# Ten node-range places in one register load on VectorE: a graph layer on one Trainium2 core

## The chip, the core and the metric

The kernel runs on one core of a Trainium2 chip. Its engines work side by side, each from an instruction stream of its own, in order: TensorE (PE in the profile, with its weight loads as PEld), VectorE (DVE), ScalarE (ACT), GpSimd (POOL), and SyncE (SP), which here only issues DMA transfers. Each engine has a sequencer that fetches its instructions. Some instructions are the sequencer's own work and never reach the engine's arithmetic: loading a number from memory into a register, register arithmetic, and tests on registers. The profile shows those of DVE under the name DVEq and doesn't count them as busy time. Engines wait for one another by semaphores.

The metric is the device time of one execution in microseconds (us), of which the median of several runs is given. The profile is of one further execution, with a span counted from its first to its last instruction.

## The reference, cut to what matters

```
Xs  = x[src]                                       # 400,000 edges, 12,500 nodes, 128 features
msg = where(edge_type == 0, Xs @ W_data.T + b_data, Xs @ W_control.T + b_control)
agg = segment_sum(msg, dst, 12500)                 # dst is sorted
x   = layernorm(x + relu(agg + (x @ W_self.T + b_self)))
```

A row of `x` is fetched for every edge, the rows are summed by destination node, separately for the two edge types, and the sums go through the weights. The kernel sums first and multiplies by the weights after, and it counts the edges of each type and node, since each brings one bias.

## The kernel before

**Tiling.** The edges come in 3125 chunks of 128, and 125 chunks make a group. There are 25 groups. A group covers some 500 destination nodes, and a group's chunks fall into five windows of 25 chunks. In a window 5 chunks are gathered: POOL issues one indirect transfer for each chunk (`msg`, line 793). The other 20 chunks are picked: `x` lies in SBUF as three bf16 parts, and TensorE fetches the edges' rows by multiplying with matrices of zeros and ones (`got`, line 893), which ACT copies to SBUF as bf16 (`emsg`, line 907). In 18 of the groups the last window is gathered as a whole, so the kernel has 107 picked sets in all, here called rounds, and 125 gathered ones.

**Summing.** TensorE multiplies the fetched rows with a selection matrix that DVE makes by comparison (`esel` for picked rows, three pieces of 1760, 1584 and 1056 columns for each round; `psel` for gathered ones; both at line 516, in the helper `select`). The product is a tile `sums` in PSUM (line 738), of which there are two. Its columns are a narrow range of destination nodes for either edge type. A tile for gathered rows also has the counts (line 824).

**Adding up.** DVE adds `sums` into `acc`, a tile of 128 x 3 x 640 fp32 for each group, at line 782 (`accumulate`). The columns of `acc` at which a window's range begins depend on the data. These are the places: ten numbers for each group, five for gathered and five for picked ranges, of which the groups with four rounds use nine. They are worked out on the chip for all groups near the start, held between 0 and 520 by a max and a min (lines 405 and 406), and lie as whole numbers in one partition of SBUF (`place_i`, `raw["place"]`). `place_of(g, i)` at lines 772 to 776 loads one of them into a register of DVE. `accumulate` uses that register as part of its addresses. A gathered window has two additions: the counts (64x120) as soon as they are there, and the sums (128x2x40 or, where all 25 chunks are gathered, 128x2x120) at the window's end. A picked round has one (128x2x88).

**The rest of DVE's round.** For the round two ahead DVE works out where its edges stand: `O` (line 516), `ahead` (613), `prod` (617, 622), `found` (624), `rank` (626), `rm` (516), `rv` (657), `key` and MAX8 (630, 634), `om_all` (541), and `pick` (724), the matrix with which TensorE picks. Once a group, index tiles are prepared (`parts`, `pk`, lines 494 to 498) and the nodes of a group that is complete are multiplied by the weights and normalized (lines 1012 to 1045). Line 766 carries the overlap of `acc` on to the next group.

**What sets the order.** `merged` and `evenly` give each piece of work a place in a round, and the pieces are recorded in that order. The layer that records them then orders the instructions of each engine anew, by what it reckons of when their operands are ready. `tc.issue_after(ins)` holds an instruction behind another of its engine in that order: a place's load stands behind the last addition but one that was recorded before it. POOL's gathers are paced by TensorE's progress (`paced`).

After the main part every engine loads one number (`bad`, line 118) and skips a slow path that covers unlikely data.

Of the kernel before, what the change touches and what calls it, by code (L numbers as in the profile page):

```python
# [39 lines left out]
WMAX = max(AW, EW)  # L40
CHUNKS = PB + EC
M0 = 50
R = 640
# [16 lines left out]
def kernel(  # L60
# [53 lines left out]
    with ExitStack() as sx:  # L114
        short_path(sx, tc, const, ident, eps, wT, brow, bad, x, src, dst, etype,
                   (w_data, w_ctrl, w_self), (b_data, b_ctrl, b_self), out)
# [89 lines left out]
def short_path(ctx, tc, const, ident, eps, wT, brow, bad, x, src, dst, etype, ws, bs, out):  # L206
    nc = tc.nc
# [32 lines left out]
    raw = {}  # L240
# [484 lines left out]
        return [(0.6, lambda: half(0, NCELL))]  # L725


    acc, added, parts_in = {}, [], {}

    def sums():  # L730
        return ps2.tile([P, 512], FP, name="sums")
# [40 lines left out]
    def place_of(g, i):  # L772

        parts_in[g] = parts_in.get(g, 0) + 1
        with tc.issue_after(added[-2].ins) if len(added) > 1 else ExitStack():
            return nc.vector.value_load(raw["place"][0:1, g, i:i + 1], min_val=0, max_val=R - WMAX)  # L776

    def accumulate(at, rows, ps, wide, width):

# [49 lines left out]
    def gathered(g, i):  # L829
# [3 lines left out]
        def add_counts():  # L833
            s["at"] = place_of(g, 2 * i)
            accumulate(s["at"], acc_rows(g, 2, 3)[:2 * CAP], s["ps"][:2 * CAP, 2 * AW:], AW, AW)
# [37 lines left out]
    def picked(w, tiled, ending, before):  # L873
# [83 lines left out]
        def end():  # L957

            early, *more = tiled.get(turns, [lambda: None])
            early()  # L960
            gates = add(bounds[turns - 1], NQ)
            for u in more:
                u()
            accumulate(place_of(g, 2 * i + 1), acc_rows(g, 0, 2), s["ps"], EW, EW)
            return gates
# [174 lines left out]
    for w in range(pairs):  # L1140
        g, i = each_e[w]
# [182 lines left out]
```

## Time and profile before

| | |
|---|---|
| time, median of 3 runs | 1736.49 us (1736.48 to 1737.98) |
| the profiled execution | 1736.82 us, span 1735.1 us |
| PE busy | 1585.6 us, 91% of the span |
| DVE busy | 1559.6 us, 90% |
| ACT busy | 1228.9 us, 71% |
| POOL busy | 1243.4 us, 72% |
| TensorE clock granted | 0.998 |
| DMA | 252.35 MB, mean 145 GB/s |

The shares are means over the whole span. The first 60 us are a start-up with little work for PE (7.63 us busy), and the last 23 us an ending (14.23 us); between them each stretch of 200 us looks like the next. A busy engine isn't one that sets the time: what bounds the kernel is read from who waits for whom. In the tables of groups, a row has the line, engine, operation, tiles and shape with the count, then the busy time in us and the mean of one in ns, then the idle time of the engine before them and what ended it. In the tables of waits a row has who waited for what, the total in us, the number of times and the longest. In the table of one line's instructions, the three numbers are the shortest, median and longest in ns.

### The profile page before, as it was taken

The numbers are of one execution on the slowest core, as the hardware profiler recorded it, in microseconds if no ns is written. First come the engines' busy times: TensorE is split into PE (matmuls) and PEld (weight loads), VectorE is DVE, ScalarE is ACT, GpSimd is POOL, SyncE is SP. The second block draws the span as 40 slices with busy tenths as digits, with TensorE's granted clock in tenths as the row PEclk, the third lists the DMA queues.
The fourth block names the chain that finished last, engine by engine and source line by source line (L and its number), as shares of the span: only waits on it lengthen the run. The fifth ranks groups of instructions, "written<-read, shape, count | busy, mean of one in ns | idle before, by whom it ended". The sixth has DMA issues, their size and how long they took to land.

```text
span 1735.1 us, 67976 instructions
## 1 busy us (share of the span) xinstructions
PE 1585.6 (91%) x28250; PEld 1249.1 (72%) x28250; DVE 1559.6 (90%) x3642; ACT 1228.9 (71%) x2201; POOL 1243.4 (72%) x1059
## 2 busy tenths in 40 slices
PE   1699999999999999999999999999999999999997
PEld 0477777777677777777777777777777777777776
DVE  7898999999999999999898999899999898999983
ACT  5777777767777676767677777776777676777675
POOL 1276778877778776767787777776777777777671
PEclk9999999999999999999999999999999999999999
DMA  7844454555454454444545444544454544444441
GB/s 221 275 135 137 130 155 127 159 153 149 124 158 130 139 159 147 134 144 135 151 125 169 138 149 130 159 130 154 139 162 124 161 129 146 146 154 126 136 134 46
DMA packets 145646, 252.35 MB, mean 145 GB/s; under 512 B 35563, under 2 KB 111936, under 8 KB 145328
## 3 DMA queue, kind: packets, MB, share of 16 engines
q1 hardware_dynamic: 82670, 138.54, 23.6%
q0 software_dynamic: 50032, 102.98, 22.3%
q10 hardware_dynamic: 12626, 6.40, 1.3%
q8 instruction: 223, 3.65, 0.9%
q14 instruction: 95, 0.78, 0.1%
HBM read 230.17 MB, written 17.67 MB: 143 GB/s over the span
## 4 chain that ended last, share of the span: by engine, by line
DVE 43%; PE 39%; issue 9%; ACT 5%; DVEq 2%; DMA 2%; SPq 0%; ACTq 0%
PE sums L738 17%; PE got L893 13%; DVE esel L516 5%; DVE prod L622 4%; DVE pick L724 3%; DVE prod L617 3%; PE side L1012 3%; DVE rv L657 3%; DVE found L624 2%; DVE psel L516 2%; DVE prod L595 2%; DVE acc L782 2%; ACT emsg L907 2%; DVE O L516 2%; DVEq L776 2%
## 5 line engine op out<-in xcount | busy, mean ns | idle before, releaser
L793 POOL DMA_INDIRECT msg<-rows,idx_g x985 | 1174.3, 1192 | 361.6 <-issue 128.6
L907 ACT CAST emsg<-got 128x768 bf16<-128x768 f32 (+1 forms) x1070 | 953.7, 931 | 360.1 <-PE got L893 338.4
L738 PE MATMUL sums<-esel,emsg 128*128 128x176 bf16 x7704 | 686.6, 240 | 0.6 <-ACT emsg L907 0.4
L738 PEld LDWEIGHTS <-emsg 128*128 128x128 bf16 x7704 | 566.0, 98 | 102.8 <-issue 95.5
L893 PE MATMUL got<-x,pick 128*32 128x384 bf16 x10486 | 584.8, 330 | 15.2 <-DVE pick L724 9.7
L893 PEld LDWEIGHTS <-pick 128*32 128x32 bf16 x10486 | 239.7, 96 | 135.0 <-DVE pick L724 12.1
L516 DVE TENSOR_TENSOR esel<-code_col,code 128x1760 bf16<-128x1760 bf16 x321 | 293.0, 913 | 16.2 <-PE sums L738 14.9
L738 PE MATMUL sums<-psel,msg 128*128 128x48 bf16 x2955 | 183.6, 184 | 31.3 <-DVE acc L782 29.3
L738 PEld LDWEIGHTS <-msg 128*128 128x128 bf16 x2955 | 153.8, 97 | 62.4 <-issue 58.3
L622 DVE TENSOR_TENSOR prod<-prod 128x1200 bf16<-128x1200 bf16 x214 | 133.7, 625 | 4.7
L516 DVE TENSOR_TENSOR O<-cell_col,blk 128x2000 bf16<-128x2000 bf16 x107 | 127.6, 1193 | 8.2 <-ACT blk L420 3.7
L617 DVE TENSOR_TENSOR prod<-O,ahead 128x2000 bf16<-128x2000 bf16 x107 | 128.4, 1200 | 5.8 <-DVE ahead L613 3.5
L782 DVE TENSOR_TENSOR acc<-acc,sums 128x80 f32 (+3 forms) x357 | 98.9, 280 | 32.4 <-PE sums L738 29.8
L516 DVE TENSOR_TENSOR psel<-near_col,near 128x1200 bf16<-128x1200 bf16 x125 | 97.4, 779 | 23.1 <-issue 22.4
L724 DVE TENSOR_SCALAR pick<-pick,lane_f 128x3200 bf16<-128x3200 bf16 x107 | 112.8, 1054 | 0.6 <-DMA pick<-there 0.6
L868 POOL DMA_INDIRECT both<-rows,idx x54 | 63.4, 1174 | 64.6 <-ACT emsg L907 27.0
L669 PE MATMUL side<-rv,O 128*128 128x64 bf16 x2140 | 83.6, 195 | 23.0 <-DVE rv L657 21.5
L669 PEld LDWEIGHTS <-O 128*128 128x128 bf16 x2140 | 78.8, 100 | 24.9 <-DVE rv L657 21.8
L657 DVE TENSOR_TENSOR rv<-rm,vals 128x1280 bf16<-128x1280 bf16 x107 | 87.8, 820 | 0.0
L624 DVE TENSOR_REDUCE found<-prod 128x20 f32<-128x600 bf16 x107 | 83.0, 776 | 5.2 <-DVE prod L622 2.7
L595 DVE TENSOR_TENSOR prod<-O 128x1000 bf16<-128x1000 bf16 x107 | 71.8, 671 | 0.0
L605 PEld LDWEIGHTS <-ltri 128*128 128x128 bf16 x1284 | 40.4, 97 | 36.3 <-issue 34.5
(171 smaller groups left out, 1536.2 us busy)
## 6 DMA issues: line engine op xcount, KB each, us to landing
pick<-there SPq DMA_DIRECT2D x106, 800.0 KB
acc<-acc_start SPq DMA_DIRECT2D x23, 960.0 KB
msg<-rows,idx_g POOLq DMA_INDIRECT x985
rows<-x SPq DMA_DIRECT2D x6, 1344.0 KB
xs<-in_x_dram SPq DMA_DIRECT2D x99, 62.5 KB
out_dram<-h SPq DMA_DIRECT2D x99, 62.5 KB
xt<-in_x_dram ACTq DMA_DIRECT2D x6, 896.0 KB
there<-cell SPq DMA_DIRECT2D x106, 6.2 KB
```

Source lines behind the costliest of these rows:

```text
L516: nc.vector.tensor_tensor(sel.rearrange("p n (w t) -> p n w t", t=2), col[:rows].rearrange("p (o w t) -> p o w t", o=1, t=2).to_broadcast( ...
L617: nc.vector.tensor_tensor(prod[:, :, :NCELL], s["O"], ahead.rearrange("p (o j) -> p o j", o=1).to_broadcast([P, EC, NCELL]), op=OP.mult,)
L622: nc.vector.tensor_add(prod[:, :, :h], prod[:, :, :h], prod[:, :, h:2 * h])
L624: nc.vector.tensor_reduce(found, prod[:, :, :h], AX.X, OP.add)
L657: placed[:] = [nc.vector.tensor_tensor(rv.rearrange("p c v (r t) -> p c v r t", t=2), rm.rearrange("p c (o r t) -> p c o r t", o=1, t=2).t ...
L669: nc.tensor.matmul(s["rk"][:m, :2 * CAP], s["held"][:, c * NCELL:c * NCELL + m], s["rv"][:, c].rearrange("p v r -> p (v r)"), start=(c == ...
L724: nc.vector.tensor_scalar(t, t, lane_f, None, op0=OP.is_equal)
L738: last = nc.tensor.matmul(out, msg[:, j * D:(j + 1) * D], sel, start=(start and j == 0), stop=stop, skip_group_check=True)
L782: added.append(nc.vector.tensor_add(win, win, ps[:, :n * wide].rearrange("p (a w) -> p a w", w=wide)[:, :, :width]))
L793: return nc.gpsimd.indirect_dma_start(out=msg, out_offset=None, in_=rows3[:, :], in_offset=bass.IndirectOffsetOnAxis(ap=codes["p", g][0][: ...
L893: last = nc.tensor.matmul(ps[CAP * a:CAP * (a + 1), :], slots[w]["pick"][:, a * NQ + q, :], x3[:, 4 * q + a - a0].rearrange("p j d -> p (j ...
L907: s["out"] = nc.scalar.copy(msg[:, :n], ps[:, :n, :3 * D])
```

## The change

`place_of` loads a group's ten places with one instruction the first time that a place of this group is asked for, and keeps the ten registers. Later calls for the group load nothing. The instructions that test at run time whether a place lies between 0 and 520 are left out. Only the first call for a group is held behind an addition, by the same rule as before. The additions and their addresses are as they were.

```diff
-    acc, added, parts_in = {}, [], {}
+    acc, added, parts_in, at_places = {}, [], {}, {}
...
     def place_of(g, i):
 
         parts_in[g] = parts_in.get(g, 0) + 1
-        with tc.issue_after(added[-2].ins) if len(added) > 1 else ExitStack():
-            return nc.vector.value_load(raw["place"][0:1, g, i:i + 1], min_val=0, max_val=R - WMAX)
+        if g not in at_places:
+            with tc.issue_after(added[-2].ins) if len(added) > 1 else ExitStack():
+                _, at_places[g] = nc.values_load_multi_w_load_instructions(
+                    raw["place"][0:1, g, :], engines=[nc.vector.engine], min_val=0, max_val=R - WMAX,
+                    skip_runtime_bounds_check_because="places are held to this range by a max and a min on the chip",
+                )
+        return at_places[g][i]
```

The lines behind the edit move down by five: what was line 782 is line 787 in the changed kernel, and the load is at line 777.

## The prediction

> **What bounds the kernel now.** First the page's head, the busy times and the chain that ended last, then two stretches of the steady part.
>
> ```profile
> span 1735.1 us, 67976 instructions
> PE 1585.6 (91%) x28250; PEld 1249.1 (72%) x28250; DVE 1559.6 (90%) x3642; ACT 1228.9 (71%) x2201; POOL 1243.4 (72%) x1059
> DVE 43%; PE 39%; issue 9%; ACT 5%; DVEq 2%; DMA 2%; SPq 0%; ACTq 0%
> PE sums L738 17%; PE got L893 13%; DVE esel L516 5%; DVE prod L622 4%; DVE pick L724 3%; DVE prod L617 3%; PE side L1012 3%; DVE rv L657 3%; DVE found L624 2%; DVE psel L516 2%; DVE prod L595 2%; DVE acc L782 2%; ACT emsg L907 2%; DVE O L516 2%; DVEq L776 2%
> ```
> ```profile
> 400.00:600.00 200.00, 188.15 (x3362) 147.08 (x3359) 181.18 (x422) 140.93 (x262) 150.53 (x126) 1.00 0.48 143
> 1000.00:1200.00 200.00, 188.24 (x3398) 148.89 (x3396) 183.80 (x422) 142.09 (x259) 151.11 (x127) 1.00 0.46 140
> ```
>
> After its length, a stretch's row gives PE, PEld, DVE, ACT and POOL. PE is busy for 188 of 200 us and DVE for 181 to 184: two engines that are both nearly full and hand work to each other. The chain takes 43% from DVE and 39% from PE, so each is the late one about as often. ACT and POOL have a quarter of their time free. The line that the change edits, L776, stands on the chain itself with 2% (about 30 us): DVE's sequencer, which fetches DVE's instructions and does the register work, loading places.
>
> Next, what DVE waited for. "<- issue" is idle time for which the profile shows no other work to wait for.
>
> ```profile
> DVE acc L782 <- PE sums L738: 29.8, 51, 1.3
> DVE ahead L613 <- PE side L605: 26.0, 48, 2.0
> DVE psel L516 <- issue: 22.4, 43, 1.5
> DVE esel L516 <- PE sums L738: 14.9, 23, 2.6
> DVE prod L617 <- DVE ahead L613: 3.5, 10, 0.7
> DVE found L624 <- DVE prod L622: 2.7, 12, 0.2
> DVE x L293 <- issue: 2.5, 1, 2.5
> DVE parts L494 <- issue: 2.3, 5, 0.5
> DVE O L516 <- issue: 2.2, 4, 0.7
> DVE rm L516 <- DVE rank L626: 1.0, 2, 0.5
> DVE acc L782 <- issue: 0.9, 2, 0.5
> ```
>
> And the reverse, PE waiting for DVE in the steady part:
>
> ```profile
> PE sums L738 <- DVE acc L782: 29.5, 53, 1.5
> PE side L545 <- DVE om_all L541: 16.8, 26, 1.6
> PE side L487 <- DVE code_r L477: 13.7, 18, 1.2
> PE got L893 <- DVE pick L724: 9.7, 13, 1.5
> ```
>
> PE's largest wait is for the addition at L782: there are two `sums` tiles in PSUM, and PE can begin a new set only when DVE has added an old one into `acc`. These rows give 69.7 us of PE waiting for DVE, against 70.7 us (29.8 + 26.0 + 14.9) of DVE waiting for PE. So I count a stall of DVE, added or taken away, at half: about half of the time the other engine would have been the late one anyway.
>
> **What goes: 232 loads and their tests.** The instructions of L776, and the address arithmetic of L782, which stays:
>
> ```profile
> L776 DVEq TENSOR_LOAD <-place_i x232: 296/304/1402, 42.1 to 1721.3; - x116
> L776 DVEq FUSED_REGOPS  x232: 183/190/206, 43.4 to 1721.7; - x116
> L776 DVEq SEQ_ASSERT  x232: 23/23/31, 43.6 to 1721.9; - x116
> L782 DVEq FUSED_REGOPS  x357: 69/75/117, 78.1 to 1722.8; - x179
> ```
>
> A place costs the sequencer 304 + 190 + 23 = 517 ns and the gaps between, in which it dispatches nothing. DVE goes on with what it has been given and then stands. What that looks like:
>
> ```profile
> 498.70 0.16 DVE L1038 SCALAR_TENSOR_TENSOR nm<-mv,rs 125x4 f32<-125x4 f32 x1
> 500.05 0.78 DVE L516 TENSOR_TENSOR psel<-near_col,near 128x1200 bf16<-128x1200 bf16 x1 [1.19 <-issue]
> ```
>
> Two places were loaded here behind one instruction of 0.16 us: 1.19 us idle, so about 0.66 us each with gaps. Over the whole kernel the idle time that fits is the issue rows (22.4 + 2.5 + 2.3 + 2.2 + 0.9 = 30.3) and the three short rows in which DVE waited for itself although a load stood between (3.5 + 2.7 + 1.0 = 7.2): 37.5 us. The ends are 0, if PE is always next, and 37.5; 2% of the chain lies between. By the half: **-19 us**. What is late next is PE's product, on which the same additions and selections wait.
>
> **What comes: 25 loads of ten.** In the order of the built program one load stands for each of the 25 groups, with no test behind it. Its price is in no row. Ends: 0.304 us, if ten registers cost what one does, and 3.04 us, if each costs the whole. I take the sequencer's shortest register instruction (the 75 ns of L782) as the share paid once and the rest of the 304 as paid per register: 0.075 + 10 x 0.229 = 2.37 us. That is nearer the upper end, because the one-register row is all but constant (296 to 304 in half of the cases, far above 75), which looks like a trip to memory and back rather than like decoding.
>
> The Trainium skill ("Runtime: NRT & Kernel Launch", section on instruction fetch mechanics) has a register load at some 200 ns per register even in bulk; by it, as an estimate, ten cost 304 + 9 x 200 = 2.1 us, and the time below would be 1750. The traced load of one register, 304 ns, fits that rule with 100 ns paid once but does not prove it.
>
> Where the new loads stand matters more. The old ones were spread over the stream; each new one is directly ahead of its group's first addition. In the built order 12 of them stand ahead of the 64x120 addition, which takes the counts out of `sums`, and 13 ahead of the 128x2x88 addition. Behind the load are queued the address arithmetic, that addition, and DVE's next selection; PE waits for the addition (the 29.5 us row). What covers a load is the instruction ahead of it:
>
> ```profile
> L516 DVE TENSOR_TENSOR O<-cell_col,blk 128x2000 bf16<-128x2000 bf16 x107 | 127.6, 1193 | 8.2 <-ACT blk L420 3.7 <-issue 2.2 <-ACT emsg L907 1.2
> L516 DVE TENSOR_TENSOR esel<-code_col,code 128x1760 bf16<-128x1760 bf16 x107 | 113.6, 1061 | 7.1 <-PE sums L738 6.7
> L516 DVE TENSOR_TENSOR esel<-code_col,code 128x1584 bf16<-128x1584 bf16 x107 | 104.3, 974 | 0.4
> L624 DVE TENSOR_REDUCE found<-prod 128x20 f32<-128x600 bf16 x107 | 83.0, 776 | 5.2 <-DVE prod L622 2.7
> L541 DVE TENSOR_SCALAR om_all<-slot_col,side 128x448 bf16<-128x448 bf16 x107 | 42.9, 440 | 1.0 <-PE side L535 0.5
> L782 DVE TENSOR_TENSOR acc<-acc,sums 128x176 f32 x107 | 35.5, 332 | 25.8 <-PE sums L738 24.9 <-issue 0.5
> L498 DVE SCALAR_TENSOR_TENSOR pk<-idx_g,vals 128x125 f32<-128x125 int32 x25 | 7.0, 280 | 0.0
> L634 DVE MAX8 top<-key 128x8 f32<-128x20 f32 x107 | 18.2, 171 | 0.6
> L516 DVE TENSOR_TENSOR esel<-code_col,code 128x1056 bf16<-128x1056 bf16 x107 | 75.3, 704 | 8.8 <-PE sums L738 8.1
> ```
>
> The built order has ahead of the loads six O, six MAX8, three found, three om_all, two pk, two selections of 1584, one of 1760, one addition of 332 ns and one tiny instruction: 7.16 + 1.03 + 2.33 + 1.32 + 0.56 + 1.95 + 1.06 + 0.33, 15.7 us over 25, or 0.63 us each. The addition would also have waited for PE for 29.8 / 357 = 0.08 us. Exposed: 2.37 - 0.71 = 1.66 us, times 25 is 41.5 us on DVE, half of it **+21 us**. The ends are 0 (at 0.304 us all is covered) and 25 x (3.04 - 0.71) = 58 us.
>
> The test of the range that is dropped was work of the sequencer only, counted above. DMA issues and the queues of SP and POOL keep their instructions; POOL's order differs in two places and SP's in some 70, with transfers loaded far ahead of use: nothing.
>
> **What moves.** Taking 232 loads out lets the layer that orders the instructions arrange all of DVE anew: beside the loads, 1524 of 4421 rows of DVE's order stand elsewhere, by up to 19 places. DVE is in order, so a row that stands ahead of its time holds everything behind it. Three shifts can be counted. The third selection (128x1056), which needs a tile that PE is still reading, stands ahead of its round's `found` in 31 rounds instead of 12, and behind the nearest `pick` in 31 instead of 18, where PE is kept waiting for it: 32 shifts. The 64x120 addition stands directly behind `rm` or `found`, well ahead of its old place, in 21 cases instead of 6. At the mean of one such wait in the rows above (14.9 / 23 = 0.65 us for a selection, 29.8 / 51 = 0.58 us for an addition) that is 32 x 0.65 + 15 x 0.58 = 29.5 us, half of it **+15 us**. A gain cannot be excluded, since the new order could as well serve PE better elsewhere; ends -15 (the same size, the other way) and +30 (passed on in full).
>
> **Sum.** -19 + 21 + 15 = +17 us on the profiled execution's 1736.82 us; the median of the runs is 1736.49, 0.3 below, so 1753.5 us, 1.0% slower.
>
> **The rivals.**
>
> *A load of ten costs little more than a load of one.* Place: the 25 loads. Then they are covered, and the sum is -19 + 15 = -4, 1733 us; with an order that costs nothing, 1718. It decides below the price at which 25 x (L - 0.71) / 2 equals 4, L = 1.03 us. For it: nothing in the trace says that the 304 ns are per register. Against: they are far above the 75 ns of pure register work. The Trainium skill ("DMA: Bandwidth & Descriptors", latency and other measured facts) gives a tensor load a floor of some 600 ns that unrolling spreads, which would speak for this rival; the trace's 304 ns is half of that floor.
>
> *The new stalls pass in full.* PE stands for just that addition, so a late one may delay PE by all of it: -19 + 41.5 + 15, 1774 us. For it: the 29.5 us row is PE's largest wait. Against: it was 53 waits in 357 additions.
>
> *The order costs nothing.* Waits change place without adding up: -19 + 21 = +2, 1739 us. For it: the counted shifts are a few among 1524.
>
> That the change does less than it says is excluded: the built program has 25 loads at that line, no tests, and the same 3642 instructions of DVE proper.
>
> **How the numbers follow.** Chances: forecast 0.55, its own range 1744 to 1766; cheap load 0.23; full passing 0.12; neutral order 0.10. Of the cheap load's 0.23, 0.13 end faster by over 0.2% (3.5 us, about what a measurement of this kernel can tell from no change), 0.06 within, 0.04 slower. The neutral order splits into 0.02, 0.05 and 0.03; of the forecast 0.01 is within. Faster 0.15, same 0.12, slower 0.73. The range from 1731 to 1774 leaves out the cheap load with a good order below (about 0.12) and part of the full passing above (0.06).
>
> **What will show it.** L776's rows shrink to 25 loads without register operations or tests; their median is the price: near 2.4 us if I am right, under 1.0 if the first rival is. The "psel <- issue" row disappears. DVE's busy sum stays at 1560. PE's wait for the addition grows from 29.5 us, DVE's wait for PE at the 128x1056 selection from 8.1 us. If both of these stay and the load is long, the order term was wrong; if DVE's idle time falls and the time with it, the half was too little for the gain.

## The result, and the profile after

The changed kernel takes 1754.96 us, the median of 4 runs (1754.22 to 1755.82), against 1736.95 us (1736.48 to 1737.98) for the kernel before: a ratio of 1.0104, 95% interval 1.0091 to 1.0118. It is about 18 us slower, and the forecast was 1753.5.

The head of the changed kernel's page and the shares of its chain by engine (the profiled execution took 1755.82 us):

```profile
span 1754.1 us, 67306 instructions
PE 1602.5 (91%) x28250; PEld 1254.1 (71%) x28250; DVE 1556.9 (89%) x3642; ACT 1229.5 (70%) x2201; POOL 1261.2 (72%) x1059
PE 43%; DVE 38%; issue 7%; ACT 5%; DMA 1%; POOL 1%; DVEq 1%; ACTq 0%; POOLq 0%
```

DVE has 2.7 us less work than before in a span that is 19 us longer, so it stands still longer: span less busy time was 175.5 us and is 197.2. The sequencer's share of the chain (DVEq) has fallen from 2% to 1%.

TensorE's row holds a surprise. Span less busy time was 149.5 us for PE and is 151.6, hardly more, while its busy time grew by 16.9 us at the same 28250 matmuls. The means of its two largest groups are as before (240 ns for the sums of picked rows, 330 ns for `got`), so the matmuls overlap less. PE takes them in another order now; the ends of matmuls are modelled in the profile, so a stall shorter than a matmul can also stand as busy time. The granted clock, 0.998 before and 0.995 after, would make some 5 us of it if the busy time went with it (0.3% of 1585.6, an estimate).

What is left at the line of the load, first all 25 of them, then three neighbours, each from a window of its own:

```profile
L777 DVEq TENSOR_LOAD <-place_i x25: 1061/2296/2629, 78.4 to 1677.8; - x25
...
L777 DVEq TENSOR_LOAD <-place_i x1: 2317/2317/2317, 1344.3 to 1344.3; - x1
L777 DVEq TENSOR_LOAD <-place_i x1: 1064/1064/1064, 1409.6 to 1409.6; - x1
L777 DVEq TENSOR_LOAD <-place_i x1: 2300/2300/2300, 1472.2 to 1472.2; - x1
```

There are 25 loads of ten registers, and no tests. But they have two prices. From the second load on they alternate all through the kernel: 2.30 us for groups 1, 3, 5 and so on, 1.07 us for 2, 4, 6. (Group 0's ten are among the cheap ones by their place; its load took 2.63 us here and 1.64 in another execution.)

What DVE waited for in the changed kernel:

```profile
DVE acc L787 <- PE sums L738: 53.6, 71, 1.9
DVE ahead L613 <- PE side L605: 29.0, 52, 2.0
DVE esel L516 <- PE sums L738: 26.1, 38, 1.9
...
DVE acc L787 <- issue: 8.8, 8, 2.4
```

"psel <- issue", 22.4 us before, is gone with the old loads. In its place the additions wait 53.6 us for PE (29.8 before) and the selections 26.1 (14.9), and 8.8 us stand as "issue" ahead of additions, in seven of the eight cases behind a new load that was not covered in full. What PE waited for:

```profile
PE sums L738 <- DVE acc L787: 41.7, 56, 1.9
...
PE side L545 <- DVE om_all L541: 9.6, 17, 1.6
```

PE's wait for the additions grew from 29.5 to 41.7 us. The groups of DVE where the idle time went, by shape (busy us, mean ns, idle before them):

```profile
L516 DVE TENSOR_TENSOR esel<-code_col,code 128x1056 bf16<-128x1056 bf16 x107 | 75.4, 705 | 19.3 <-PE sums L738 18.1 <-PE side L487 0.7 <-PE got L898 0.3
L516 DVE TENSOR_TENSOR psel<-near_col,near 128x1200 bf16<-128x1200 bf16 x125 | 96.3, 770 | 0.0
L787 DVE TENSOR_TENSOR acc<-acc,sums 128x176 f32 x107 | 35.7, 333 | 46.4 <-PE sums L738 37.4 <-PE got L898 5.6 <-issue 2.9
L787 DVE TENSOR_TENSOR acc<-acc,sums 64x120 f32 x125 | 32.9, 263 | 11.7 <-issue 5.9 <-PE sums L738 3.1 <-PE side L690 2.4
```

The means are within about one per cent of those before. The 128x1056 selection now stands 19.3 us idle (8.8 before), the 128x176 addition 46.4 (25.8).

### The profile page after: what moved, and what is told of

Same layout as the page of the kernel before. It is cut to its first block, busy times and chain, and to the rows that moved or that the text cites. A ratio compares the mean times of both kernels' runs of the same rounds, so it can differ in the third digit from the quotient of the medians.

```text
span 1754.1 us, 67306 instructions
## 1 busy us (share of the span) xinstructions
PE 1602.5 (91%) x28250; PEld 1254.1 (71%) x28250; DVE 1556.9 (89%) x3642; ACT 1229.5 (70%) x2201; POOL 1261.2 (72%) x1059
## 4 chain that ended last, share of the span: by engine, by line
PE 43%; DVE 38%; issue 7%; ACT 5%; DMA 1%; POOL 1%; DVEq 1%; ACTq 0%; POOLq 0%
PE sums L738 19%; PE got L898 13%; DVE esel L516 5%; PE side L1017 4%; DVE prod L622 4%; DVE pick L724 3%; DVE rv L657 3%; DVE found L624 3%; DVE prod L617 2%; ACT emsg L912 2%; DVE psel L516 2%; DVE prod L595 2%; DVE acc L787 2%; DVE rm L516 2%; PE side L605 2%
## 5 line engine op out<-in xcount | busy, mean ns | idle before, releaser
L798 POOL DMA_INDIRECT msg<-rows,idx_g x985 | 1189.0, 1207 | 358.6 <-issue 132.3
L738 PE MATMUL sums<-esel,emsg 128*128 128x176 bf16 x7704 | 695.0, 240 | 2.7 <-DVE acc L787 1.9
L516 DVE TENSOR_TENSOR esel<-code_col,code 128x1760 bf16<-128x1760 bf16 x321 | 293.4, 914 | 27.5 <-PE sums L738 26.1
L787 DVE TENSOR_TENSOR acc<-acc,sums 128x80 f32 (+3 forms) x357 | 99.5, 280 | 71.4 <-PE sums L738 53.6
L605 PEld LDWEIGHTS <-ltri 128*128 128x128 bf16 x1284 | 41.2, 97 | 34.9 <-issue 32.5
```

The lines of the kernel that those rows point to most:

```text
L516: nc.vector.tensor_tensor(sel.rearrange("p n (w t) -> p n w t", t=2), col[:rows].rearrange("p (o w t) -> p o w t", o=1, t=2).to_broadcast( ...
L738: last = nc.tensor.matmul(out, msg[:, j * D:(j + 1) * D], sel, start=(start and j == 0), stop=stop, skip_group_check=True)
L787: added.append(nc.vector.tensor_add(win, win, ps[:, :n * wide].rearrange("p (a w) -> p a w", w=wide)[:, :, :width]))
L798: return nc.gpsimd.indirect_dma_start(out=msg, out_offset=None, in_=rows3[:, :], in_offset=bass.IndirectOffsetOnAxis(ap=codes["p", g][0][: ...
```

## The experiments

They ran on three chips. The kernel before takes 1738.34 us on chip C, which is like the chip of the profiles above, but 2005.22 us on chip A and 2001.79 us on chip B. There TensorE now and then stands with nothing to wait for that the trace shows, and waits longer for the other engines; the mean times of its two largest groups differ by about one per cent. So each ratio is to the kernel before on the same chip, and ratios are set side by side only with the chip named. The changed kernel as it is was timed on the first chip and on chip C, not on A or B.

**What one load costs (chip B).** Loads of several sizes and places, at the end of the kernel before:

```diff
+    with tc.issue_after(added[-1].ins):
+        for k in range(0, 200, 40):
+            use(load_n(flat[:, k + 0:k + 1], **on))
...
+            use(load_n(flat[:, k + 2:k + 12], **on))
...
```

> The kernel before, with 70 register loads of VectorE added at its end, each followed by one small addition that uses its first register: 1, 2, 4, 8, 10 and 16 registers in one instruction, beginning 0, 1, 2 or 3 words behind a multiple of 16 bytes, five of each. If the place in memory sets the price: 304 ns for one register wherever it lies, 1.07 us for ten at 0 words, 2.30 us for ten at 2 words, and about 85 ns or 222 ns for each further register. If ten registers have two prices for another reason (an alternation from one load to the next), the prices will not sort by place. The additions at the end change acc after its last use, and no output.

The rows of the added lines, in order: one register at 0 words behind a multiple of 16 bytes and at 1; two at 0; four at 0 and at 2; eight at 0 and at 2; ten at 0, 1, 2 and 3; sixteen at 0. Shortest, median and longest in ns:

```profile
L1197 DVEq TENSOR_LOAD <-place_i x5: 313/319/320, 1993.7 to 2067.1; - x5
L1198 DVEq TENSOR_LOAD <-place_i x5: 301/309/310, 1994.9 to 2067.7; - x5
L1199 DVEq TENSOR_LOAD <-place_i x5: 534/536/537, 1995.4 to 2068.2; - x5
...
L1202 DVEq TENSOR_LOAD <-place_i x5: 358/358/365, 1997.9 to 2070.5; - x5
L1203 DVEq TENSOR_LOAD <-place_i x5: 961/961/962, 1998.4 to 2071.0; - x5
L1204 DVEq TENSOR_LOAD <-place_i x5: 608/609/614, 1999.6 to 2072.2; - x5
L1205 DVEq TENSOR_LOAD <-place_i x5: 1839/1839/1846, 2000.4 to 2073.0; - x5
L1206 DVEq TENSOR_LOAD <-place_i x5: 1076/1077/1083, 2002.5 to 2075.1; - x5
L1207 DVEq TENSOR_LOAD <-place_i x5: 2283/2283/2283, 2003.8 to 2076.4; - x5
L1208 DVEq TENSOR_LOAD <-place_i x5: 2283/2283/2291, 2006.3 to 2079.3; - x5
L1209 DVEq TENSOR_LOAD <-place_i x5: 2279/2283/2283, 2008.8 to 2081.6; - x5
L1210 DVEq TENSOR_LOAD <-place_i x5: 1101/1103/1104, 2011.3 to 2084.0; - x5
```

Place decides. Off the multiple of 16 bytes each further register costs about 219 ns: (2283 - 309) / 9, where 309 is the median of one register at 1 word. On it, each further four together cost about 250 ns: (609 - 358) and (1103 - 609) / 2. Only what is left over is paid one by one: ten at 0 are eight (609) and two singles, 1077 in all, hardly less than sixteen. A group's ten numbers fill 40 bytes, so every second group begins 8 bytes off. My expectation of 85 ns a register in aligned loads was a mean over quads and singles.

**Aligned rows, and the old order (chip A).** Four kernels. The first pads the rows:

```diff
-        place_i = raw["place"] = keep.tile([1, NG, NWIN], I32, name="place_i")
+        place_i = raw["place"] = keep.tile([1, NG, 12], I32, name="place_i")[:, :, :NWIN]
```

The others add order edges at the end of the recording, along a list of the instructions as the other kernel issues them. Register loads and their arithmetic stay free; a load of ten then stands ahead of its group's first addition, as in the changed kernel.

```diff
     ending()
     for u in rest + last:
         u()
+    keep_order(tc, nc)
...
+def keep_order(tc, nc):
...
+            if prev is not None:
+                tc.add_manual_dep(
+                    ins[at], prev.name,
+                    mybir.DependencyInfo(mybir.DependencyClass.NoSync, mybir.DependencyReason.DATA), reason="order",
+                )
+            prev = ins[at]
```

> The changed kernel with place_i laid out in rows of 12 numbers instead of 10, so that each group's ten begin at a multiple of 16 bytes. In the changed kernel's trace the load of ten took about 2.30 us for the odd groups, whose ten begin 8 bytes behind such a multiple, and 1.065 us for the even ones. The order of every engine's instructions is that of the changed kernel. If the place in memory sets the price, all 25 loads take about 1.07 us, the exposed part falls by 12 x 1.23 = 15 us, and by my half the time falls by 7 us to about 1747 (1739 if it passes in full). If something else that alternates from group to group sets the price, the loads stay at two prices and the time at 1755. If the order of the instructions is all that counts, the loads fall to 1.07 us and the time stays at 1753 to 1755.

> The changed kernel, its loads as they are, with the instructions of VectorE, TensorE and ScalarE issued in the order that the kernel before has. My prediction has the changed order at +15 us (bounds -15 and +30): by it the time is 1755 - 15 = 1740, and 1725 if the order passes in full. The rival that the order costs nothing gives 1755, unchanged. The waits of PE for the addition should go back from 41.7 us toward 29.5, and the idle time of DVE ahead of the 128x1056 selection from 19.3 us toward 8.8.

> Both edits: rows of 12 numbers, and the instructions in the order of the kernel before. If loads and order are terms that add up, as in my sum, the time is 1755 - 7 - 15 = 1733, a little faster than the kernel before. If the gain of the 232 removed loads passes in full and the loads of 1.07 us are nearly covered, 1737 - 30 = 1707 is the lower end. If taking the loads away is worth nothing because TensorE is always next, it is the time of the kernel before, 1737.

> The kernel before, with its 232 loads of one place and their range tests, and the instructions of VectorE, TensorE and ScalarE issued in the order of the changed kernel. This measures the order by itself: my prediction gives 1737 + 15 = 1752 (ends 1722 and 1767); the rival that the order costs nothing gives 1737. A load's place in the stream may differ by a few instructions from where it stood before, which I count at nothing.

| chip A | old order | new order |
|---|---|---|
| 232 loads with tests | 2005.22 (the kernel before) | 2032.65, ratio 1.0137 (1.0114 to 1.0159) |
| 25 loads, unaligned | 2000.32, ratio 0.9987 (0.9965 to 1.0009) | not run here |
| 25 loads, aligned | 1993.46, ratio 0.9948 (0.9930 to 0.9967) | 2030.30, ratio 1.0147 (1.0121 to 1.0173) |

The load's row with aligned rows in the new order:

```profile
L777 DVEq TENSOR_LOAD <-place_i x25: 1061/1066/1315, 85.2 to 1946.1; - x25
```

All 25 are cheap now. In the old order that saves 2000.32 - 1993.46 = 6.9 us of the 12 x 1.23 = 15 that the loads fall by. That is about the half, but with intervals of some 4 us on either time it could be nearly nothing or nearly all. The order costs 27 us with the old loads and 37 with aligned ones, on this chip well above my +15 and near or above its end of +30. The rival that the order costs nothing is out. Nor do the terms simply add up: in the new order the aligned loads take no more off than the old loads do (1.0147 and 1.0137), in the old order they take off 12 us. PE's wait for the additions, aligned loads in the old order and then in the new:

```profile
PE sums L738 <- DVE acc L787: 27.3, 46, 1.6
```
```profile
PE sums L738 <- DVE acc L787: 46.9, 60, 3.0
```

**Tests without grouping, and one shift undone (chip B).** The second kernel here drops the tests and keeps the 232 loads; with the tests gone, the loads also come out closer to their additions:

```diff
-            return nc.vector.value_load(raw["place"][0:1, g, i:i + 1], min_val=0, max_val=R - WMAX)
+            _, (at,) = nc.values_load_multi_w_load_instructions(
+                raw["place"][0:1, g, i:i + 1], engines=[nc.vector.engine], min_val=0, max_val=R - WMAX,
+                skip_runtime_bounds_check_because="places are held to this range by a max and a min on the chip",
+            )
+            return at
```

The third is the changed kernel with the list of its own order, in which the 128x1056 selections are moved back:

```diff
+    keep_order(tc, nc)
```

> The same kernel as in the first comparison of the old order (ten places in one load, unaligned, the instructions in the order of the kernel before), since the chip of that comparison ran the kernel before in 2005 us instead of 1737, with TensorE matmuls longer and the chain 60% TensorE's. On a chip that gives 1737 for the kernel before, my sum (order +15 of the +17) has it at 1740, ratio 1.002; what the slower chip showed, 0.9987, would be 1735; a neutral order would give the changed kernel's ratio again, 1.0104.

> The kernel before with its 232 loads of one place each, but without the range tests. Its instructions come out in exactly the order of the kernel before, and the loads stand directly ahead of their additions. It separates the tests from the grouping. If the exposed work of the sequencer is what costs (0.66 us for a place, of which the tests are 213 ns and some of the gaps), most of the 37.5 us of idle time goes and half of it shows: 1737 - 12 to 19, 1718 to 1725, ratio 0.989 to 0.993. If TensorE is always next, the ratio is 1.000. If a load directly ahead of an addition costs more than one that stands early, it is above 1.

> The changed kernel in its own order, with one thing undone: the 107 selections of 128x1056 stand on VectorE behind the same instructions as in the kernel before. My order term has 32 x 0.65 = 21 us of waits for this shift, half of it 10 us in the time: 1745, ratio 1.0045. If this shift is the whole of the order's cost, the ratio falls to that of the kernel with the old order; if the cost lies elsewhere in the 1500 rows that moved, or in TensorE's order, it stays at 1.010. The idle time of VectorE ahead of the 128x1056 selection should fall from 19.3 us toward 8.8 in either case.

Ten in one load in the old order: 1995.86 us, ratio 0.9975 (0.9961 to 0.9988). One by one without tests: 1992.38, 0.9955 (0.9938 to 0.9973). So leaving out the tests is worth 9 us on this chip, together with the new places of the loads, and less than the 12 to 19 that I expected. It needs no new order: VectorE's other instructions stay where they were. The grouping is what rearranged them, and in the old order it brings no more than the dropped tests do.

The undone shift brought nothing back that could be seen: 2042.09 us, ratio 1.0208 (1.0183 to 1.0233), where the kernels in the new order on chip A have 1.0137 and 1.0147. Its row of the selection:

```profile
L516 DVE TENSOR_TENSOR esel<-code_col,code 128x1056 bf16<-128x1056 bf16 x107 | 75.5, 706 | 31.9 <-PE sums L738 16.0 <-PE got L898 7.6 <-remote 3.5
```

The same row in the new order of chip A (aligned) has 36.3 us of idle time, in the old order 24.1. The selection waits somewhat less than in the aligned kernel, and the 64x120 addition more (35.3 us against 27.4). That may be a wait that moved along the queue. It is not shown, since the chip and the price of the loads differ too, and with the old loads in the new order the selection waits 32.2 us, the same as here.

**The terms one by one (chip C).** Four kernels: the changed one itself; with the list for VectorE alone; with the list for TensorE alone; and, in the old order on all three engines, with one load in all:

```diff
-        if g not in at_places:
+        if not at_places:
...
-                _, at_places[g] = nc.values_load_multi_w_load_instructions(
-                    raw["place"][0:1, g, :], engines=[nc.vector.engine], min_val=0, max_val=R - WMAX,
+                _, at_places[0] = nc.values_load_multi_w_load_instructions(
+                    raw["place"][0:1, 0, :], engines=[nc.vector.engine], min_val=0, max_val=R - WMAX,
...
-        return at_places[g][i]
+        return at_places[0][i]
```

> The changed kernel itself, on the chip of the other comparisons, which gives about 2003 us for the kernel before. There its own order with aligned loads had a ratio of 1.0147, and in the old order the unaligned loads cost 0.3 to 0.4% more than the aligned ones (0.9975 and 0.9987 against 0.9948). If loads and order add up, the ratio is 1.018; if the unaligned loads are hidden in the new order, 1.0147; if the order costs there what it costs on the first chip, 1.010.

> The changed kernel with VectorE's instructions alone put in the order of the kernel before; TensorE's and ScalarE's are left to the layer that orders them, which gives TensorE an order that is neither that of the kernel before nor that of the changed one. My prediction put the cost of the order on VectorE (selections and additions that stand ahead of their time). If so, the ratio is that of the kernel with all three engines in the old order, 0.998. If TensorE's order carries it, the ratio stays near 1.015. In between means that the two orders belong together.

> The other half: TensorE's instructions alone in the order of the kernel before, VectorE's and ScalarE's left free, by which VectorE's order comes out close to that of the changed kernel (622 of 3642 rows elsewhere, against 1407 from the order before). If VectorE's order carries the cost, the ratio stays at 1.015; if TensorE's does, it falls to 0.998.

> The old order on all three engines, with one load of ten registers in the whole kernel: every group adds at the places of the first group, so the sums of all other groups land in wrong columns; the instructions and their sizes are the same. It leaves out 24 of the 25 loads, and with them all waiting for registers. By the measured prices the loads expose 13 x (2.30 - 0.71) + 12 x (1.07 - 0.71) = 25 us; by my half the time falls by 12 us, from a ratio of 0.998 to 0.992; in full, to 0.986; if the loads are hidden in the old order, it stays at 0.998.

| chip C | us | ratio (interval) | step |
|---|---|---|---|
| the kernel before | 1738.34 | | |
| one load in all, old order | 1720.40 | 0.9890 (0.9875 to 0.9905) | 232 loads and tests out: -17.9 |
| 25 loads, VectorE in the old order | 1740.18 | 1.0011 (1.0002 to 1.0020) | loads of ten in: +19.8 |
| the changed kernel | 1755.38 | 1.0094 (1.0079 to 1.0109) | VectorE's own order: +15.2 |
| 25 loads, TensorE in the old order | 1786.81 | 1.0292 (1.0271 to 1.0313) | |

The expectations came from chip A; chip C turned out to be like the first one. The changed kernel has its ratio of there again, not 1.018. VectorE's old order takes back most of what the changed kernel lost, as my prediction had it, though not down to 0.998. Between the one-load kernel and the next row lie 19.8 us, between my half (12) and the full 25.

Only the first step is clean, since all three engines have the order of the kernel before there. In the third row TensorE and ScalarE have an order of their own, so the second and third steps hold a change of it too. The heads of the two pages, the one-load kernel (span 1720.4 us) and VectorE in the old order (1736.8 us), show that this counts:

```profile
PE 1585.1 (92%) x28250; PEld 1249.5 (73%) x28250; DVE 1556.8 (90%) x3642; ACT 1229.0 (71%) x2201; POOL 1260.1 (73%) x1059
```
```profile
PE 1596.5 (92%) x28250; PEld 1248.1 (72%) x28250; DVE 1556.5 (90%) x3642; ACT 1231.2 (71%) x2201; POOL 1247.7 (72%) x1059
```

Of the 16.4 us between the spans, 11.4 are busy time of PE and only 5.0 idle time. In the first step, where TensorE kept its order, its busy time stayed (1585.6 before, 1585.1). So how much of the 19.8 us the loads cost, and how much TensorE's order, is open. PE's wait for the additions in the one-load kernel, the kernel with VectorE in the old order, and the changed kernel:

```profile
PE sums L738 <- DVE acc L787: 16.1, 35, 1.3
```
```profile
PE sums L738 <- DVE acc L787: 32.5, 47, 1.9
```
```profile
PE sums L738 <- DVE acc L787: 41.6, 55, 1.9
```

This row rises by 16.4 us in the second step, in which PE's other waits shrink, and by 9.1 with VectorE's new order. In the one-load kernel, where no load stands in the way, DVE's largest waits are for PE:

```profile
DVE acc L787 <- PE sums L738: 43.8, 68, 3.0
DVE ahead L613 <- PE side L605: 32.6, 58, 1.4
```

TensorE's old order with an order of VectorE close to the changed kernel's is the slowest of all, by 31 us over the changed kernel. PE's waits there:

```profile
PE sums L738 <- DVE acc L787: 44.6, 54, 2.6
PE side L487 <- DVE code_r L477: 27.8, 18, 3.6
...
PE got L898 <- DVE pick L724: 14.2, 14, 4.1
```

It waits 27.8 us for `code_r` (7.5 in the changed kernel) and 14.2 for `pick` (5.7): TensorE's order asks for tiles that VectorE's order makes later. The two orders belong together, and this mixture is worse than either. The other one, VectorE's old order with a TensorE left free, is faster than the changed kernel (1740.18 us).

## Why the prediction was right

**What goes.** Forecast -19, measured -17.9 (by the interval -16.5 to -21.7). The idle rows that I tied to the loads, 37.5 us, went away and about half of it showed. The cause was the one named, PE next in line: with the loads gone DVE waits 43.8 us for PE ahead of its additions (29.8 before, on the first chip) and 32.6 ahead of `ahead` (26.0). PE's wait for the additions fell by 13.4 us (29.5 to 16.1), nearly all that the span lost (14.7).

**What comes.** Forecast +21, measured +19.8 in a step that also holds a new order of TensorE; the agreement is no proof of the term. The price of 2.37 us, 75 ns once and 229 for each register, is close to what an unaligned load costs (2.30 us). It does not hold for the aligned half, at 1.07. By measured prices the exposed part is 12 x (2.30 - 0.71) + 13 x (1.07 - 0.71) = 24 us, not 41.5; the 0.71 us of cover is still my estimate from the built order. If all 19.8 us were the loads', some 80% of that passed into the time and the step "half of it" was too low. But 11.4 of the 16.4 us by which the span grew stand in PE's busy time, not in a wait for an addition. The runs that kept the old order on all three engines point lower: with ten in one load they are 4.9 us (chip A) and 5.9 us (chip B) faster than the kernel before, where my two terms gave +2. Set against the -17.9 of chip C, that leaves 12 to 13 us for the loads, the half of 24. This goes across chips and is an estimate. So the price of the aligned half was wrong for certain; whether the half was wrong as well stays open between 50% and 80%. The wait on which I built the term did grow, PE standing for the additions (16.1 us without the loads, 32.5 with them and another order of TensorE). The rule of the Trainium skill ("Runtime: NRT & Kernel Launch", instruction fetch mechanics), some 200 ns a register even in bulk, agrees with the unaligned loads (219 ns), though the page speaks of loads from HBM and the places lie in SBUF; for aligned ones four registers cost about 250 ns together.

**What moves.** Forecast +15, measured +15.2 for VectorE's order on chip C, and 27 to 37 us for all three engines' on chip A. By the same estimate across chips the whole order costs 22 to 23 us on chip C. That the order costs was right, and that it costs through PE's wait for the additions in good part (9.1 of the 17.0 us that the span grew in this step). The shifts that I counted for the size were not shown to carry it: with the 128x1056 selection put back, nothing was gained. The cost lies in how VectorE's order as a whole meets TensorE's, and which of the moved rows weigh most stays open. Putting the 64x120 additions back in the same way was not tried. The agreement to 0.2 us is luck, and so in part is that of the sum: if the loads cost 12 to 13 us and the order 22 to 23, the one term was too high by about as much as the other was too low.

**The rivals.** The cheap load was right for every second group: 1.07 us, just above the 1.03 from which it would decide. With aligned rows all 25 would have that price; the order term alone would still have kept the changed kernel slower, as on chip A. Stalls that pass in full (1774) are not shown; the 19.8 us would come near, but of a smaller sum than 41.5, and they hold TensorE's order too. The neutral order is refuted by the old loads in the new order on chip A (1.0137).

**What was to be seen.** It came as said, but for the price: "psel <- issue" vanished, DVE's busy sum stayed (1556.9 against 1559.6), PE's wait for the addition and DVE's at the 128x1056 selection grew (29.5 to 41.7, 8.1 to 18.1). The median load was 2.30 us, near the 2.4 named, but stands for half of the loads only.

## What to carry to other kernels

Removing instructions that only the sequencer handles can rearrange everything else: list the new order before counting the gain, and fix the old order by edges to measure the two apart, on every engine whose order moves. Here the old order with aligned loads was faster than the kernel before (0.9948 on chip A) and dropping the tests was too (0.9955 on chip B), while the change as made is slower (1.0104 and 1.0094 on the other two chips). A register load that stands directly ahead of the instruction on which another engine waits can cost the time a good part of what is exposed, by the estimates above half or more; place and align it with that in mind.

## What the runs showed of the hardware

That a register load of VectorE is priced by its alignment was not expected: 1.08 us for ten registers from a multiple of 16 bytes, 2.28 us from 4, 8 or 12 bytes behind one, and 0.36 against 0.96 us for four. By these rows twelve aligned registers should cost 609 + 250 = 0.86 us, less than ten, by an estimate that no run tested.

And chips differ in what the same program waits for. On chip A, in the kernel with aligned loads in the old order, PE stood with nothing to wait for that the trace shows, which is nearly absent on the faster chips, and longer for ACT:

```profile
PE got L898 <- ACT emsg L912: 47.1, 78, 3.8
...
PE sums L738 <- issue: 21.3, 63, 1.5
...
PE got L898 <- issue: 19.0, 53, 1.3
```

The first of these rows is 4.7 us in the kernel before on the first chip. That it is the chip and not the kernel shows in the run with the added loads on chip B, whose main part is the kernel before:

```profile
PE got L896 <- ACT emsg L910: 44.7, 73, 1.7
```

What makes these chips 15% slower is not settled by these rows. The granted clock, 0.983 in this execution on chip A against 0.998 on the first chip, is lower by 1.5%.
